# Two graph layers on one core: the softmax maxima taken over 2048 keys per head chosen on chip, and one exp over two PSUM banks

## The chip, the cores and the metric

The kernel runs on one core of a Trainium2 chip. The metric is the device time of one execution in microseconds (us). The median of three runs of the kernel before is 13,376.75 us (13,372.65 to 13,378.7). The profile shows one execution, whose span is 13,361.7 us. The engines are called PE (matrix products), DVE (vector engine), ACT (activations such as exp), POOL (GpSimd) and SP (which here only issues DMAs). PSUM, where PE writes, has eight banks of 512 float32 values on each of 128 partitions.

## The reference

Two layers run over a graph of N = 3327 nodes with 128 features. The first multiplies by the normalised adjacency matrix and its transpose and normalises. The second is attention with 128 heads of 8 dimensions, and it is nearly all of the time:

```python
q = (x @ Wq.T).reshape(d, n, h)          # d = 128 heads, n = 3327, h = 8
k = (x @ Wk.T).reshape(d, n, h)
v = (x @ Wv.T).reshape(d, n, h)
a = jnp.einsum('dnh,dmh->dnm', q, k) * scale
a = a + spatial_encoding + edge_encoding  # both are adj
a = jax.nn.softmax(a, axis=2)
out = jnp.einsum('dnm,dmh->dnh', a, v)
out = out.reshape(n, h * d)
return out @ Wo.T
```

The adjacency matrix has about five nonzero entries in a row, so it changes few scores. Its result is added to the input and normalised.

## The kernel before

**Stages.** The first layer comes first. A projection stage then makes q, k and v, 13 tiles of 256 nodes, and writes them to device memory. q and k are split into three bfloat16 parts each, stacked on 48 rows, so that one bfloat16 matmul gives the product in nearly full precision. Then comes the attention loop, and last a stage that joins results, multiplies by Wo and normalises.

**The attention loop.** Heads are taken in 32 groups of four (`g`), queries in seven blocks of 512 (`b`; the last has 255), and keys in 26 tiles of 128 (`t`). For each (g, b, t) and head a matmul (line 757) gives scores, `e_ps`, keys on partitions and queries along the bank; ACT takes exp of one bank (line 767) into `es`; and a float32 matmul (line 725) adds `es` times v into `o`. In the code the four heads are taken in two turns of the loop over `j0`; I call such a turn a half. For the last block of 255 queries, one turn takes all four heads, two to a bank.

**The maxima.** exp needs the maximum of each query's scores over all keys. A generator, `maxima()`, computes them some 76 items ahead of the exps. One item is a two-bank matmul pair (line 557), queries on partitions, and a DVE maximum over its 1024 scores (line 579). A row tile of 128 queries has 13 items for the four heads, among them two heads whose first 768 keys are stored as half sums and half differences, so that max(a, b) comes from an absolute value on ACT (line 567) and a sum on DVE (line 573). One item is taken per half. Scores use rows 0 to 49 of PE, maxima rows 64 to 111.

**From maximum to exp.** When a block's maxima are done, `lowest` (lines 516 to 528) reduces them on DVE and POOL splits the result into two bfloat16 numbers, `two`. `turn()` counts items; TURN items later `to_queries` transposes `two` on DVE (line 533), and SP stores it and loads it under the block's queries as two more rows, to be subtracted by the score matmul.

**The neighbours.** The scores above leave out adj. Beside the loop, `neighbours()` treats each node's up to 16 neighbours on POOL: 26 row tiles of nodes, each with 16 steps over keys (one indirect gather of 128 rows, line 605, and the products of lines 645 to 651), ten short steps and 16 steps over values (a gather and lines 690, 691). `by_node()` before it reorders the tables with DMAs, 256 steps. One step of the two is taken after every PACE = 4 rounds of `t`.

**Order.** Inside the loop the order of instructions on PE, ACT, DVE, POOL and SP is the order in which the code emits them (`manual_schedule`, line 702). Each engine works through its own list and stops at an instruction whose operands are not ready.

```python
            if total % PACE == 0:
                next(beside, None)
```

Of the kernel before, what the change touches and what calls it, by code (L numbers as in the profile page):

```python
# [20 lines left out]
P = 128  # L21
N = 3327
# [18 lines left out]
CW = 10  # L41
# [8 lines left out]
LEAD = 38  # L50
TURN = 8
MIXED = (0, 2)
PAIRED = 768
HALF = PAIRED // 2
SLOTS_MX = 6


def paired_from(head):

    return -head * N % (2 * D)  # L60
# [7 lines left out]
def gnn_layers(ctx: ExitStack, tc: tile.TileContext, x, adj, adjt, w_in, w_out, wq, wk, wv, wo, out):  # L68
# [10 lines left out]
    x1 = const.tile([P, NT, D], F32, name="x1")  # L79
# [10 lines left out]

    kk_d = dram.tile([2 * PARTS * H, G // 2], BF16, name="kk_d")
# [6 lines left out]
    ones_d = dram.tile([2, NP], BF16, name="ones_d")  # L98
    negmax_d = dram.tile([NG * len(BLOCKS), 2, GH * NB], BF16, name="negmax_d")
# [23 lines left out]
    with ExitStack() as c0:  # L123
# [4 lines left out]
        with ExitStack() as c1:  # L128
            first = c1.enter_context(tc.tile_pool(name="first", bufs=1))
            x0 = first.tile([P, NT, D], F32, name="x0")  # L130
            nc.sync.dma_start(x0, x.rearrange("(t p) d -> p t d", p=P))
# [107 lines left out]
            with tc.tile_pool(name="ps_mix", bufs=2, space=PSUM) as ps_mix:  # L239
# [4 lines left out]
                apply_norm(x0, stats, small, lambda t: x1[:, t, :])  # L244
                for t0 in range(0, NT, 4):
# [18 lines left out]
                most = small.tile([P, 1], F32, name="most")  # L264
                nc.vector.reduce_max(most, over, axis=AX.X)
                mark = small.tile([P, 1], F32, name="mark")
                nc.vector.tensor_scalar(mark, most, 0.0, None, op0=ALU.is_gt)
                ones = small.tile([P, 1], F32, name="ones")
                nc.vector.memset(ones, 1.0)
                marks = ps_mix.tile([1, 1], F32, name="marks", bufs=1)  # L270
                nc.tensor.matmul(marks, mark, ones, start=True, stop=True)
                nc.vector.tensor_copy(bad, marks)


# [8 lines left out]
        def load_group(g):  # L283
# [4 lines left out]
            for slot, parts in KROWS:  # L288
                src = heads[: H * parts].rearrange("r (j n) -> r j n", j=GH)
                pairs.append((k[H * slot : H * slot + H * parts, :, :N], src))  # L290
                rows = slice(64 + H * slot, 64 + H * slot + H * parts)
                for j in range(GH):
                    if j not in MIXED:
                        pairs.append((k[rows, j, :N], src[:, j]))
                        continue

                    n0 = paired_from(g * GH + j)
                    n1 = n0 + PAIRED + NB - HALF
                    at = ((g * GH + j) * N + n0) // 2
# [735 lines left out]
```

## Time and profile before

| what | value |
|---|---|
| median of three runs | 13,376.75 us |
| profiled execution, span | 13,361.7 us |
| projection stage to first maxima | 438 to 836 us |
| first maxima to last output copy | 836 to 13,121 us |
| of it the loop with exps | 924 to 13,121 us |
| last stage | 13,121 to 13,361.7 us |
| busy over the span: PE, DVE, ACT, POOL | 95%, 96%, 94%, 39% |

In a group line of the profile, "x" and a number is a count, then follow the busy time in us and the mean duration of one instruction in ns, and after the bar the idle time of the engine ahead of it and what ended it. In a timeline line the first number is the start in us and the second the length. Instructions of one engine overlap at their ends, so the step from start to start can be shorter than the length of one. A line of the table of waits has the engine, tile and line that waited, what it waited for, and the total in us, the count and the longest.

### The profile page before, as it was taken

The numbers are of one execution on the slowest core, as the hardware profiler recorded it, in microseconds if no ns is written. First come the engines' busy times: TensorE is split into PE (matmuls) and PEld (weight loads), VectorE is DVE, ScalarE is ACT, GpSimd is POOL, SyncE is SP. The second block draws the span as 40 slices with busy tenths as digits, with TensorE's granted clock in tenths as the row PEclk, the third lists the DMA queues.
The fourth block names the chain that finished last, engine by engine and source line by source line (L and its number), as shares of the span: only waits on it lengthen the run. The fifth ranks groups of instructions, "written<-read, shape, count | busy, mean of one in ns | idle before, by whom it ended". The sixth has DMA issues, their size and how long they took to land.

```text
span 13361.7 us, 325240 instructions
## 1 busy us (share of the span) xinstructions
PE 12748.4 (95%) x131844; PEld 3270.1 (24%) x131844; DVE 12885.2 (96%) x17679; ACT 12532.3 (94%) x24146; POOL 5245.4 (39%) x4554
## 2 busy tenths in 40 slices
PE   7669999999999999999999999999999999999996
PEld 3312222222222222222222222222222222222224
DVE  9779999999999999999999999999999999999996
ACT  6549999999999999999999999999999999999994
POOL 0310000004555555555555555555555555554100
PEclk8869999999999999999999999999999999999997
DMA  6753333333334443343434433434433344443203
GB/s 236 200 117 31 31 33 31 30 33 61 64 65 74 73 71 66 68 70 64 65 67 68 66 66 67 72 70 69 68 68 67 68 70 68 64 66 63 37 9 110
DMA packets 2622120, 929.24 MB, mean 70 GB/s; under 512 B 2265088, under 2 KB 2473096, under 8 KB 2613946
## 3 DMA queue, kind: packets, MB, share of 16 engines
q1 hardware_dynamic: 2488794, 398.26, 25.1%
q0 software_dynamic: 127920, 465.26, 12.7%
q10 hardware_dynamic: 3888, 44.82, 0.9%
q8 instruction: 1035, 16.96, 0.6%
q14 instruction: 483, 3.96, 0.1%
HBM read 786.21 MB, written 150.74 MB: 70 GB/s over the span
## 4 chain that ended last, share of the span: by engine, by line
PE 79%; DVE 14%; ACT 3%; DMA 2%; issue 1%; SPq 1%; POOL 0%; DVEq 0%; ACTq 0%; POOLq 0%
PE o L725 39%; PE m L557 35%; DVE mx L579 9%; PE e_ps L757 4%; ACT es L767 2%; DVE larger L573 1%; PE acc L191 1%; DMA q_d<-parts 1%; DVE top_at L201 1%; DVE top_w L200 1%; PE y L809 1%; DVE mx L571 0%; SPq L344 0%; ACT o_sb L734 0%; ACT size L567 0%
## 5 line engine op out<-in xcount | busy, mean ns | idle before, releaser
L767 ACT ACTIVATE es<-e_ps 128x512 f32<-128x512 f32 x21632 | 11447.8, 612 | 197.4 <-PE e_ps L757 126.5
L579 DVE TENSOR_REDUCE mx<-m 128x1 f32<-128x1024 f32 (+3 forms) x10816 | 10874.1, 1071 | 77.2 <-PE e_ps L757 40.2
L757 PE MATMUL e_ps<-q_st,k_st 50*128 50x512 bf16 (+1 forms) x23296 | 6661.1, 366 | 87.0 <-ACT es L767 78.8
L557 PE MATMUL m<-k_st,q_st 48*128 48x512 bf16 (+1 forms) x23296 | 6508.5, 366 | 164.1 <-DVE mx L579 84.8
L725 PE MATMUL o<-es,v 128*9 128x256 f32 (+1 forms) x83456 | 6626.7, 389 | 5.5 <-ACT o_sb L734 5.4
L557 PEld LDWEIGHTS <-q_st 48*128 48x128 bf16 x23296 | 1417.8, 94 | 5068.9 <-issue 4126.7
L725 PEld LDWEIGHTS o<-es,v 128*9 128x9 f32 x83456 | 1243.1, 88 | 4214.1 <-issue 4191.3
L526 POOL CAST two<-nm 128x16 bf16<-128x16 f32 (+1 forms) x224 | 44.1, 197 | 5621.7 <-DVE nm L520 5502.4
L757 PEld LDWEIGHTS <-k_st 50*128 50x128 bf16 (+1 forms) x23296 | 1400.2, 95 | 148.3 <-issue 112.0
L645 POOL TENSOR_TENSOR prod<-qn,near_rows 128x1024 f32<-128x1024 f32 x416 | 987.1, 2373 | 33.1 <-DMA q_st<-q_d 16.2
L573 DVE CUSTOM_DVE_ANT_0 larger<-size,m 128x384 f32<-128x384 f32 x1664 | 914.6, 550 | 66.0 <-PE e_ps L757 60.9
L567 ACT ACTIVATE size<-m 128x384 f32<-128x384 f32 x1664 | 809.6, 487 | 106.7 <-PE m L557 46.7
L691 POOL TENSOR_TENSOR acc<-acc,prod 128x1024 f32<-128x1024 f32 x390 | 887.8, 2276 | 30.6
L690 POOL TENSOR_TENSOR prod<-near_rows,s 128x1024 f32<-128x1024 f32 x390 | 772.8, 1982 | 6.8
L647 POOL TENSOR_TENSOR half<-prod 128x512 f32<-128x512 f32 x416 | 530.6, 1276 | 32.6
L571 DVE TENSOR_REDUCE mx<-m 128x1 f32<-128x128 f32 x1664 | 472.6, 284 | 27.0 <-ACT size L567 10.3
L605 POOL DMA_INDIRECT near_rows<-kn_d,near x416 | 419.0, 1007 | 112.2 <-issue 53.1
L605 POOL DMA_INDIRECT near_rows<-vn_d,near x416 | 413.4, 994 | 61.5 <-issue 16.9
L191 PE MATMUL acc<-a_t,x 128*128 128x512 f32 (+1 forms) x728 | 310.6, 583 | 63.3 <-DMA a_t<-in_adj_dram 43.3
L674 POOL TENSOR_TENSOR s<-s,gain 128x2048 f32<-128x2048 f32 x26 | 93.9, 3610 | 682.6 <-ACT s L673 682.6
L649 POOL TENSOR_TENSOR quarter<-half 128x256 f32<-128x256 f32 x416 | 254.9, 613 | 32.6
L189 ACT ACTIVATE unread<-a_t 128x3327 bf16<-128x3327 f32 x52 | 155.0, 2980 | 103.6 <-PE acc L191 38.3
(154 smaller groups left out, 3399.8 us busy)
## 6 DMA issues: line engine op xcount, KB each, us to landing
q_st<-q_d SPq DMA_DIRECT2D x2304, 32.0 KB
a_t<-in_adj_dram ACTq DMA_DIRECT2D x13, 1663.5 KB
a_t<-in_adj_dram SPq DMA_DIRECT2D x13, 1663.5 KB
a_t<-in_adjt_dram SPq DMA_DIRECT2D x13, 1663.5 KB
a_t<-in_adjt_dram ACTq DMA_DIRECT2D x13, 1663.5 KB
q_d<-parts SPq DMA_DIRECT2D x13, 1536.0 KB
k_d<-parts SPq DMA_DIRECT2D x13, 1536.0 KB
k_st<-k_d SPq DMA_DIRECT2D x32, 623.8 KB
```

Source lines behind the costliest of these rows:

```text
L557: nc.tensor.matmul(m[:, at : at + width], q[64 : 64 + KR, j, i * P : (i + 1) * P], k[64 : 64 + KR, j, c0 : c0 + width], start=True, stop=True,
L567: taken = nc.scalar.activation(sizes[-1][0], m[:, :HALF], AF.Abs)
L573: nc.vector.tensor_tensor_reduce(larger, size, m[:, :HALF], scale=1.0, scalar=LOWEST, op0=ALU.add, op1=ALU.max, accum_out=dst[0])
L579: reduced = nc.vector.tensor_reduce(dst[1] if kind == "sums" else dst[0], src, axis=AX.X, op=ALU.max)
L605: nc.gpsimd.indirect_dma_start(rows.rearrange("p d h -> p (d h)"), None, table, bass.IndirectOffsetOnAxis(ap=near[:, t, i : i + 1], axis=0))
L645: nc.gpsimd.tensor_mul(prod, qn, kg)
L647: nc.gpsimd.tensor_add(half, prod[:, :, :4], prod[:, :, 4:])
L690: nc.gpsimd.tensor_mul(prod, vg, share)
L691: nc.gpsimd.tensor_add(acc[:, :, :H], acc[:, :, :H], prod)
L725: nc.tensor.matmul(o[32 * j : 32 * j + VW, c : c + w], v4[:pt, j, t, :], e[j][:pt, c : c + w], start=t == 0, stop=t == NT - 1,)
L757: nc.tensor.matmul(bank[:pt, j, :w], k[: KR + 2, j0 + y * per + j, t * P : t * P + pt], q[: KR + 2, j0 + y * per + j, :w], start=True, sto ...
L767: nc.scalar.activation(es[:pt, :, :w], bank[:pt, :, :w], AF.Exp, scale=2.0)
```

## The change

The maxima of a head are taken over at most 2048 of its 3327 keys, those of largest norm. A squared norm per key is computed in the projection stage on POOL and stored (`size_d`). `select` halves an interval ten times on DVE, each time counting how many norms of each head lie above its middle, until at most 2048 are above; then matmuls with a triangular matrix give each chosen key its rank, and the others a place from the end, so that all 3327 keys get different places (`place_d`). `scatter` writes each head's float32 keys to their places in `kept_d` by indirect DMAs from POOL, 128 rows each, 104 to a group. The first eight heads are selected inside the projection stage, and the first group is scattered there; all 128 heads are selected at the start of the loop, one step per two halves, and the other groups are scattered beside the loop.

`parts_of_kept` loads a group's first 2048 places, splits them into bfloat16 parts on POOL, and items of kind "parts" transpose them on PE and copy them on DVE into `k_kept`. A maxima item is now one matmul for each of two heads, in rows 0 and 64, each with one bank, and two DVE maxima of 512. A row tile has eight items instead of 13; they are spread evenly over the halves. The half sums and differences are gone.

Scores of two heads also stand in rows 0 and 64, in two banks of one tile, and one exp covers both banks. The queries are loaded twice with heads placed accordingly (`q_m`, `q_e`). Score tiles go from three of one bank to two of two; maxima tiles from two of two banks to three of one. LEAD is 49 and TURN 5.

For every query `reach` times the largest left-out norm (`least`) bounds a left-out score; the last stage compares it with the maximum found (`short`) on POOL. The flag that chooses the general path is computed at the end of the last stage instead of after the first layer. x1 is stored in device memory and loaded again for the last stage.

```diff
+LEAD = 49
+TURN = 5
+KEPT = 2048
+KCUTS = KEPT // NB
+HALVINGS = 10
+SLACK = 1.001
+FIRST = 8
...
+            for y in range(2):
+                for slot, parts in KROWS:
+                    r = 64 * y + H * slot
+                    src = heads[: H * parts].rearrange("r (x y n) -> y r x n", y=2, n=N)[y]
+                    pairs.append((k[r : r + H * parts, :, :N], src))
...
+            both = [q_pool[0].tile([P, 2, NB], BF16, name=name, bufs=n) for name, n in (("q_m", 3), ("q_e", 4))]
...
+        def select(pool, bank, first_head, n, store):
+
+            sizes = pool.tile([n, NP], F32, name="sizes")
+            nc.vector.memset(sizes[:, N:], -1.0)
+            nc.sync.dma_start(sizes[:, :N], size_d[first_head * N : (first_head + n) * N].rearrange("(h n) -> h n", n=N))
+            cuts = [slice(c, c + NP // 4) for c in range(0, NP, NP // 4)]
...
+            for _ in range(HALVINGS):
+                nc.vector.tensor_scalar(middle, low, high, 0.5, op0=ALU.add, op1=ALU.mult)
+                for c, cut in enumerate(cuts):
+                    nc.vector.tensor_scalar(
+                        above, sizes[:, cut], middle, None, op0=ALU.is_gt, op1=ALU.add, accum_out=count[:, c : c + 1]
+                    )
+                    yield
...
+                turned = bank()
+                for x in range(nt):
+                    nc.tensor.matmul(turned[:, x * n : (x + 1) * n], chosen[:, x, :], ident_b[:n, :n], start=True, stop=True)
...
+        def load_choice(pool, s):
+
+            at = pool.tile([P, NT, GH], U32, name="at", bufs=2)
+            keys = pool.tile([P, GH, NT, H], F32, name="keys", bufs=2)
+            nc.sync.dma_start(at, place_d[:, s])
+            for j in range(GH):
+                head = (s * GH + j) * N
+                nc.sync.dma_start(keys[:, j], kf_d[head : head + NP, :].rearrange("(p t) h -> p t h", t=NT))
+            return at, keys
+
+        def scatter(s, at, keys):
+
+            for t in range(NT):
+                n = P if t < NT - 1 else P - 1
+                for j in range(GH):
+                    nc.gpsimd.indirect_dma_start(
+                        kept_d[s * GH + j],
+                        bass.IndirectOffsetOnAxis(ap=at[:n, t, j : j + 1], axis=0),
+                        keys[:n, j, t, :],
+                        None,
+                    )
+                    yield
...
-            def mixed_keys(s, full, sb):
...
+                            square = stage.tile([P, H, D], F32, name="square", bufs=1)
+                            nc.gpsimd.tensor_mul(square, full, full)
+                            for h in (4, 2, 1):
+                                nc.gpsimd.tensor_add(square[:, :h], square[:, :h], square[:, h : 2 * h])
+                            nc.gpsimd.dma_start(size_d[g].rearrange("(p s c) -> p s c", p=P, s=2)[:, s], square[:, 0])
...
+                if t == 0:
+                    for _ in select(chooser, lambda: ps_pr.tile([P, H * D], F32, name="pr"), 0, FIRST, store_first):
+                        pass
+                    scattered = scatter(0, *load_choice(chooser, 0))
+                elif t > 2:
+                    for _ in range(12):
+                        next(scattered, None)
...
-        ps_e = c1.enter_context(tc.tile_pool(name="ps_e", bufs=3, space=PSUM))
-        ps_m = c1.enter_context(tc.tile_pool(name="ps_m", bufs=2, space=PSUM))
+        ps_e = c1.enter_context(tc.tile_pool(name="ps_e", bufs=2, space=PSUM))
+        ps_m = c1.enter_context(tc.tile_pool(name="ps_m", bufs=3, space=PSUM))
...
+            kept = side.tile([P, GH * KEPT // P, H], F32, name="kept")
+            for j in range(GH):
+                nc.sync.dma_start(
+                    kept[:, j * KEPT // P : (j + 1) * KEPT // P, :],
+                    kept_d[s * GH + j][:KEPT, :].rearrange("(p t) h -> p t h", p=P),
+                )
...
+            nc.gpsimd.tensor_copy(parts[:, :, 0], kept)
+            nc.gpsimd.tensor_sub(left, kept, parts[:, :, 0])
+            nc.gpsimd.tensor_copy(parts[:, :, 1], left)
+            nc.gpsimd.tensor_sub(parts[:, :, 2], left, parts[:, :, 1])
+            for to, of in ((3, 0), (4, 1), (5, 0)):
+                nc.gpsimd.tensor_copy(parts[:, :, to], parts[:, :, of])
+            yield parts
...
+                                yield "maxima", g, q, mx, i, x, c
+                    late.append([1, lowest, (g, b, q_e, mx)])
+                    if b == len(BLOCKS) - 1 and g + 1 < NG:
+                        for c in range(KCUTS):
+                            for x in range(2):
+                                turn()
+                                yield "parts", g + 1, parts, x, c
...
+        def run_item(kind, g, of, *where):
+
+            banks = [ps_m.tile([P, NB], F32, name="m") for _ in range(2)]
+            kept = k_kept[g % 2]
+            if kind == "parts":
+                x, c = where
+                for y in range(2):
+                    r = slice(64 * (1 - y), 64 * (1 - y) + KR)
+                    for n in range(NB // P):
+                        at = (2 * x + y) * (KEPT // P) + c * (NB // P) + n
+                        nc.tensor.matmul(
+                            banks[y][r, n * P : (n + 1) * P],
+                            of[:, at].rearrange("p s h -> p (s h)"),
+                            ident_b,
+                            start=True,
+                            stop=True,
+                        )
...
+            mx, i, x, c = where
+            for y in range(2):
+                r = slice(64 * (1 - y), 64 * (1 - y) + KR)
+                nc.tensor.matmul(
+                    banks[y], of[r, x, i * P : (i + 1) * P], kept[r, x, c * NB : (c + 1) * NB], start=True, stop=True
+                )
...
+            for y in range(2):
+                nc.vector.tensor_reduce(mx[:, i, 2 * x + y, c : c + 1], banks[y], axis=AX.X, op=ALU.max)
...
+        def scatters():
+            loaded = load_choice(side, 1)
+            yield from scatter(1, *loaded)
+            yield "first"
+            loaded = load_choice(side, 2)
+            for s in range(2, NG):
+                now = loaded
+                for n, _ in enumerate(scatter(s, *now)):
+                    if n == GH * NT // 2 and s + 1 < NG:
+                        loaded = load_choice(side, s + 1)
+                    yield
...
+                reach = side.tile([P, HEADS], F32, name="reach")
+                prod = side.tile([P, HEADS, H], F32, name="prod", bufs=2)
+                nc.gpsimd.tensor_mul(prod, qn, qn)
...
+                nc.gpsimd.tensor_mul(acc[:, :, H + 2], reach, least)
...
+            steps = NG * NT * (2 * len(BLOCKS) - 1)
+            items = NG * (sum(-(-w // P) for _, w in BLOCKS) + 1) * 2 * KCUTS
...
+                        for x0 in range(0, 2, per):
+                            halves += 1
+                            bank = ps_e.tile([P, 2, NB], F32, name="e_ps")
+                            for x in range(per):
+                                for y in range(2):
+                                    r = slice(64 * y, 64 * y + KR + 2)
                                     nc.tensor.matmul(
-                                        bank[:pt, j, :w],
-                                        k[: KR + 2, j0 + y * per + j, t * P : t * P + pt],
-                                        q[: KR + 2, j0 + y * per + j, :w],
+                                        bank[:pt, y, x * NB // per : x * NB // per + w],
+                                        k[r, x0 + x, t * P : t * P + pt],
+                                        q[r, x0 + x, :w],
                                         start=True,
                                         stop=True,
                                     )
-                                banks.append(bank)
-                            for bank in banks:
-                                es = probs.tile([P, per, NB // per], F32, name="es")
+                            m = iter(())
+                            if taken * steps < halves * items:
+                                taken += 1
+                                m = next_item()
+                                next(m, None)
+                            es = probs.tile([P, 2, NB], F32, name="es")
+                            shape = "p y (x c) -> p y x c"
+                            if per == 1:
                                 nc.scalar.activation(es[:pt, :, :w], bank[:pt, :, :w], AF.Exp, scale=2.0)
-                                e += [es[:, j, :] for j in range(per)]
-                                next(m, None)
...
+                            if halves % 2 == 0:
+                                next(choosing, None)
+                            if halves <= GH * NT + 1 or (halves > 2 * GH * NT + 64 and put * 20 < 9 * (halves - 2 * GH * NT - 64)):
+                                put += halves > GH * NT + 1
+                                next(scattering, None)
...
+        nc.gpsimd.tensor_sub(short[:pt, t, :], n_t[:pt, :, H + 2], limit[:pt, 1])
...
+        nc.vector.tensor_scalar(mark[:, 0:1], most, worst, 0.0, op0=ALU.max, op1=ALU.is_gt)
```

## The prediction

> **What bounds the kernel now.** I read the page's first part, then the stretches, then the attention loop's own instructions, then GpSimd and its waits. Columns of the stretch row: its bounds and length in us, busy time of PE, weight loads, DVE, ACT, POOL, then PE clock, DMA share and GB/s.
>
> ```profile
> PE 12748.4 (95%) x131844; PEld 3270.1 (24%) x131844; DVE 12885.2 (96%) x17679; ACT 12532.3 (94%) x24146; POOL 5245.4 (39%) x4554
> ```
> ```profile
> 924.00:13121.00 12197.00, 12014.29 (x129887) 2895.61 (x129885) 11948.05 (x16276) 11998.22 (x23612) 5078.67 (x4379) 1.00 0.37 58
> ```
>
> The loop is 12,197 of 13,362 us, and PE, DVE and ACT are each 98% busy in it; POOL is 42% busy. So the loop has three limits close together, and each must be priced. I count in *halves*: one turn of the inner `j0` loop. There are 832 row tiles (26 per group, 32 groups) with 13 maxima items each, so 832 x 13 = 10,816 halves (the 21,632 exps are two per half); 12,197 / 10,816 = 1.128 us per half.
>
> DVE: one row tile's items start at 6003.59 and the next tile's at 6017.90, 14.31 us with DVE busy throughout; 832 x 14.31 = 11,906, plus its other work. It is the present pacemaker. PE is right behind (engine PE alone, start and length):
>
> ```profile
> 6000.29 0.39 PE L557 MATMUL m<-k_st,q_st 48*128 48x512 bf16 x1
> 6000.29 0.39 PE L757 MATMUL e_ps<-q_st,k_st 50*128 50x512 bf16 x1
> 6000.52 0.38 PE L557 MATMUL m<-k_st,q_st 48*128 48x512 bf16 x1
> 6000.52 0.38 PE L757 MATMUL e_ps<-q_st,k_st 50*128 50x512 bf16 x1
> 6000.83 0.62 PE L725 MATMUL o<-es,v 128*9 128x256 f32 x8
> 6001.38 0.39 PE L557 MATMUL m<-k_st,q_st 48*128 48x512 bf16 x1
> ```
> ```profile
> 13042.21 0.60 PE L757 MATMUL e_ps<-q_st,k_st 50*128 50x512 bf16 x2
> 13042.75 0.62 PE L725 MATMUL o<-es,v 128*9 128x256 f32 x8
> 13043.30 0.39 PE L757 MATMUL e_ps<-q_st,k_st 50*128 50x512 bf16 x1
> ```
>
> A maxima matmul on rows 64 up and a score matmul on rows 0 up start together. Steps: 0.225 to the next pair, 0.305 more to the products, 0.55 for those: 1.085 us. At the end, where no maxima are left, a half still takes 1.09: two score matmuls on the same rows run one behind the other. So what counts is *slots* of 512 columns, each holding one matmul on either set of rows.
>
> **What the change saves.** Both score matmuls of a half now share one slot (heads on rows 0 and 64), and so do the two of a maxima item. A half without an item costs 1.085 - 0.225 = 0.86, one with an item 1.085. Items fall from 13 to 8 per row tile: 6656, of which 49 run before the loop.
>
> PE: 10,816 x 0.86 = 9302; 6607 x 0.225 = 1487. Added: 248 "parts" items in the loop (eight turning matmuls each), no such row; eight weight loads at 94 ns and one more 0.085 mode gap (0.305 - 0.22) say 0.8 us, bounds 0.4 and 1.2: 198. The maxima get three one-bank buffers for two-bank items, so the second matmul of an item waits for the first reduce of the item just before: 0.225 + 0.38 (matmul) + 0.05 + 0.68 (reduce) + 0.06 = 1.39 against its turn at 1.31, 0.08 to 0.09 us. With items in 64% of halves this occurs in 0.28 of them: 10,816 x 0.28 x 0.09 = 271 (0 if the reduces are early, double if they lag). The 224 output copies and neighbour exps delaying ACT, about 100; block edges, 67. Sum 11,425, or **1.056 us per half**.
>
> ```profile
> L767 ACT ACTIVATE es<-e_ps 128x512 f32<-128x512 f32 x19200 | 10166.2, 613 | 157.7 <-PE e_ps L757 105.1 <-PE m L557 6.8 <-PE o L725 2.0
> L579 DVE TENSOR_REDUCE mx<-m 128x1 f32<-128x512 f32 x1664 | 1133.2, 681 | 15.9 <-PE e_ps L757 8.6 <-PE m L557 7.0
> L806 ACT COPY ot<-tr 128x1024 f32<-128x1024 f32 x25 | 25.0, 999 | 17.1 <-PE tr L804 17.1
> ```
>
> ACT: twelve exps fill 6010.43 to 6016.65, 0.518 each, 0.095 under their 613 ns. No exp of 1024 is in the trace; the nearest row, a two-bank copy, has 999, so 0.905 per half, 9790 us; at twice the present step, which is the most, 11,205. I take the row: hidden under PE. DVE: 13,312 reduces of 512 at 681 less the overlap, about 0.59, is 7854; 512 copies of kept keys at 0.6, 307; other 300: 8460, hidden. While the selection for all heads runs (about 40 passes of 832 columns in 192 halves, one per two halves), DVE needs 0.64 x 1.18 + 0.46 = 1.21 per half: +30.
>
> **What it puts on POOL.** GpSimd gets 31 x 104 indirect scatters in the loop, about 3224, each 128 rows. Their price is that of the gathers, also 128 rows each (first POOL view: three in a row; second: one step of the neighbour loop; third: one of its value loop).
>
> ```profile
> 3066.88 1.04 POOL L605 DMA_INDIRECT near_rows<-kn_d,near  x1 [45.06 <-PE o L725]
> 3068.22 0.97 POOL L605 DMA_INDIRECT near_rows<-kn_d,near  x1 [0.30 <-issue]
> 3069.49 0.95 POOL L605 DMA_INDIRECT near_rows<-kn_d,near  x1 [0.30 <-issue]
> ```
> ```profile
> 6000.57 1.01 POOL L605 DMA_INDIRECT near_rows<-kn_d,near  x1 [0.15 <-issue]
> ...
> 6007.14 1.01 POOL L605 DMA_INDIRECT near_rows<-kn_d,near  x1 [0.16 <-issue]
> ```
> ```profile
> 6214.78 0.98 POOL L605 DMA_INDIRECT near_rows<-vn_d,near  x1
> 6215.77 1.99 POOL L690 TENSOR_TENSOR prod<-near_rows,s 128x1024 f32<-128x1024 f32 x1
> 6217.83 2.28 POOL L691 TENSOR_TENSOR acc<-acc,prod 128x1024 f32<-128x1024 f32 x1
> 6220.26 0.99 POOL L605 DMA_INDIRECT near_rows<-vn_d,near  x1
> ```
>
> Busy 1.0 us, 1.27 to 1.34 from start to start, 1.15 to 1.20 beside other work: I take 1.2, bounds 1.0 and 1.3. Against it stands the Trainium skill, "DMA: Bandwidth & Descriptors", "Anatomy of one DMA": about 2.0 us fixed per GpSimd DMA, mostly completion. The rows show POOL going on after 1.3 at most, so I charge 1.2; what 2.0 gives is rival C.
>
> POOL's average would fit: 5079 + 3224 x 1.2 is under 11,425. But the scatters run at 9 per 20 halves, from half 272 to about 7205, and the neighbour work begins after 256 steps of four row steps, 7.43 halves each: half 1902. In these 5303 halves both are on POOL's queue, which is in written order. One neighbour row tile takes 43 steps, 320 halves. Other new POOL work is the kept keys' seven copies per group and the maxima's `two` pair, 0.036 per half, and a squared query per row tile, 5.5. In the key loop (16 steps, 119 halves) POOL needs 16 x 6.57 + 5.5 + 119 x (0.45 x 1.2 + 0.036) = 179 us where PE needs 119 x 1.056 = 126. In the value loop (119): 85 + 69 = 154 against 126. Between (82): 14 + 47 = 61, PE's 87 counts.
>
> What waits for POOL: `two` of each block is queued behind the scatters and steps; DVE's transposition of it (L533) is written TURN + 1 = 6 items later, some 9 us. Past that slack DVE stands, its reduces do not free banks, and PE, in order, stands at the next maxima matmul with scores and products behind it. Before, POOL was the one to wait there:
>
> ```profile
> POOL two L526 <- DVE nm L520: 5502.4, 212, 60.9
> ```
>
> So a row tile takes 179 + 154 + 87 - 9 (the slack, used once) = 411 us for PE's 338: 73 x 16.6 tiles = **+1204**.
>
> **The rest.** Projection stage (438 to 836, DMA share 0.91): mixed keys leave (3.9 us of DVE and two 1.04 casts on ACT, 26 times, with their POOL sums), but the first eight heads' selection stands in the queues after the first tile (some 40 passes near 0.93 and small steps, about 80 us), and squares, their store and twelve scatters make 33 us of POOL per tile for nine tiles where 30 is now spent: +80, bounds 0 and +150. First kept keys, +20. At the end x1 back, the limit on idle POOL and the last test: +10. SP: queries become 24 loads per block for 12, plus `kept`, `at` and `keys` loads and both result rows; near 48 issues at 0.5 us in a block of 53, hidden; nothing if it is not late, 5 us per block if a load waits for its scatter.
>
> Sum: 13,362 - 12,197 + 11,425 + 30 + 1204 + 110 = 13,934; the median of the runs is 15 over the span: **13,950 us**, slower by 4.3%.
>
> **Rivals.** *A, POOL never late:* the loop is PE's, 11,455: 12,745. It needs POOL's lag to be carried over a whole row tile and a scatter under 0.81 us ((204 + 5.5 + 320 x 0.036 + 144c) / 320 = 1.056). For it: a 32-byte row might be cheaper to describe than a 4 KB one; against: same count of rows. Where lag is not carried, break-even with before is c = 0.88 us: that one price decides the sign. *B, partly carried:* POOL's average of 1.23 counts, 5303 x 0.175 = 928, about 13,670; with c = 1.0, 451 and 13,200. *C, completion waits:* 2.0 per scatter gives 222 + 197 + 91 - 9 = 501 per tile, 15,440.
>
> That the last test fails and the general path runs I leave out: worked out from the reference's inputs, every query's kept maximum is at least 1.03 times its limit.
>
> **Chances.** Main case 0.57 (own range 13,550 to 14,350), A 0.18, B 0.15 with half of it on each side, C 0.05, others 0.05. Faster 0.28, within 0.2% 0.03, slower 0.69; 0.2% is about what a measurement tells from no change. The range leaves out half of A and what lies above: 12,750 to 14,400.
>
> **What would show it.** Right: scores of a half starting together; halves of 0.86 and 1.085 outside the overlap; long waits of DVE `turned` for POOL, POOL near 100% from some 3000 to 9800 us, then a faster stretch. Wrong: POOL idle before `two` throughout, scatters well under 0.88 or near 2 us, an exp above 1.05, or PE waiting often on maxima banks.

## The result and the profile after

The changed kernel takes 14,328.4 us (median of four runs, 14,319.2 to 14,334.8) against 13,374.7 for the kernel before on the same chip: ratio 1.0703, 95% interval 1.0685 to 1.0721. The forecast was 13,950, with a range of 12,750 to 14,400. The profiled execution of the kernel after spans 14,317.5 us. First its engines, busy time and share of the span, and the chain that ended last:

```profile
PE 12124.2 (85%) x124066; PEld 2962.0 (21%) x124066; DVE 9738.1 (68%) x16126; ACT 11235.4 (78%) x11615; POOL 9234.4 (64%) x8439
...
PE 48%; POOL 31%; issue 6%; DMA 3%; DVE 2%; ACT 2%; SPq 0%; POOLq 0%; ACTq 0%; DVEq 0%
```

Every engine that bounded the kernel before has less to do: DVE went from 12,885 to 9738 us, ACT from 12,532 to 11,235, PE from 12,748 to 12,124. No engine is near its span, and POOL, 64% busy over all, has 31% of the chain. An average doesn't tell where; stretches do. The columns are the bounds and length in us, then busy time and count of PE, weight loads, DVE, ACT and POOL, then the granted PE clock, the DMA share and GB/s. The first stretch lies ahead of the neighbours, the second is the stretch where the neighbours' work and the scatters share POOL.

```profile
1500.00:3000.00 1500.00, 1480.11 (x16238) 340.80 (x16236) 1160.71 (x1900) 1426.38 (x1469) 705.65 (x746) 1.00 0.42 35
3157.00:10284.00 7127.00, 5633.56 (x59422) 1259.35 (x59419) 4292.41 (x7029) 5241.43 (x5437) 5861.76 (x5297) 0.89 0.40 58
```

In the first PE is 99% busy, in the second 79%, with a granted clock of 0.89. The wide exps, one per half, count the halves: 1440 from 1500 to 3000, which is 1.042 us each; 5262 from 3157 to 10,284, 1.354 each; 2982 from 10,284 to 13,420, 1.052 each. These are the counts for ACT's exps (stretch, length, busy time and count, clock, DMA share, GB/s):

```profile
3157.00:10284.00 7127.00, 5169.42 (x5262) 0.89 0.40 58
10284.00:13420.00 3136.00, 2925.23 (x2982) 1.00 0.45 70
```

So nearly all of the loss sits in the middle stretch. POOL's busy share there looks like 82%, but the 0.3 us between two scatters isn't counted as busy. In this stretch POOL is busy for 5862 us, spends 778 between one indirect transfer and the next for "issue", and waits for other engines and for transfers for only some 330 in all. On its own timeline (start, length, then the idle time before and what ended it) there is no room; this is one step of the key loop, and further on the last scatters of a group:

```profile
5018.72 1.05 POOL L452 DMA_INDIRECT kept_d<-keys,at  x1 [0.16 <-issue]
5020.07 0.99 POOL L452 DMA_INDIRECT kept_d<-keys,at  x1 [0.30 <-issue]
5021.36 0.97 POOL L452 DMA_INDIRECT kept_d<-keys,at  x1 [0.31 <-issue]
5022.64 0.97 POOL L452 DMA_INDIRECT kept_d<-keys,at  x1 [0.30 <-issue]
5023.92 0.98 POOL L729 DMA_INDIRECT near_rows<-kn_d,near  x1 [0.30 <-issue]
5024.91 2.39 POOL L777 TENSOR_TENSOR prod<-qn,near_rows 128x1024 f32<-128x1024 f32 x1
...
5260.46 2.54 POOL L452 DMA_INDIRECT kept_d<-keys,at  x1 [0.30 <-issue]
```

A scatter takes 1.27 to 1.30 us from start to start, and the ones that move 127 rows (the last row tile of nodes, four per group of heads) take 2.53 to 2.71 and 0.3 more. Who waits for POOL is in the table of waits (total us, times, longest):

```profile
POOL two L632 <- DVE nm L626: 2058.6, 114, 65.5
ACT es L909 <- PE e_ps L894: 1555.2, 693, 47.2
DVE turned L639 <- POOL two L633: 1442.4, 85, 48.2
PE m L681 <- DVE mx L686: 1357.1, 146, 45.9
```

The first row is POOL's own wait. The other three are one wait seen three times: DVE stands at the transposition for `two`, PE at the next maxima matmul for DVE, ACT at the exp for PE. POOL's own wait for the maxima fell from 5502 us to 2059, nearly all of it outside the middle stretch. The other rows that answer to those of before, the exp, the reduce and the scatter in place of nothing (busy us and mean ns, then idle time before and what ended it):

```profile
L909 ACT ACTIVATE es<-e_ps 128x1024 f32<-128x1024 f32 (+1 forms) x9984 | 9803.4, 1024 | 1936.2 <-PE e_ps L894 1555.2
L686 DVE TENSOR_REDUCE mx<-m 128x1 f32<-128x512 f32 x13312 | 8330.2, 684 | 2526.4 <-PE m L681 2511.9
L452 POOL DMA_INDIRECT kept_d<-keys,at x3328 | 3508.4, 1054 | 1116.0 <-issue 894.4
```

And PE's instructions where POOL isn't late, to be held against the halves of the prediction:

```profile
2202.04 0.39 PE L894 MATMUL e_ps<-q_e,k_st 50*128 50x512 bf16 x2
2202.27 0.38 PE L681 MATMUL m<-k_kept,q_m 48*128 48x512 bf16 x2
2202.58 0.62 PE L858 MATMUL o<-es,v 128*9 128x256 f32 x8
2203.13 0.39 PE L894 MATMUL e_ps<-q_e,k_st 50*128 50x512 bf16 x2
2203.36 0.44 PE L681 MATMUL m<-k_kept,q_m 48*128 48x512 bf16 x2
2203.73 0.62 PE L858 MATMUL o<-es,v 128*9 128x256 f32 x8
2204.28 0.39 PE L894 MATMUL e_ps<-q_e,k_st 50*128 50x512 bf16 x2
2204.60 0.62 PE L858 MATMUL o<-es,v 128*9 128x256 f32 x8
2205.16 0.39 PE L894 MATMUL e_ps<-q_e,k_st 50*128 50x512 bf16 x2
```

Two score matmuls start together (x2), the maxima pair 0.23 later, the products 0.31 after that: 1.09 us from 2202.04 to 2203.13. The half that begins at 2204.28 has no item and takes 0.88. In the one at 2203.13 the second matmul of the item is late by 0.06, the wait for a bank.

### The profile page after: what moved, and what is told of

The parts are those of the page before. It is cut to its first block, busy times and chain, and to the rows that moved or that the text cites. A ratio compares the mean times of both kernels' runs of the same rounds, so it can differ in the third digit from the quotient of the medians.

```text
span 14317.5 us, 309098 instructions
## 1 busy us (share of the span) xinstructions
PE 12124.2 (85%) x124066; PEld 2962.0 (21%) x124066; DVE 9738.1 (68%) x16126; ACT 11235.4 (78%) x11615; POOL 9234.4 (64%) x8439
## 3 DMA queue, kind: packets, MB, share of 16 engines
q0 software_dynamic: 238080, 483.48, 14.3%
## 4 chain that ended last, share of the span: by engine, by line
PE 48%; POOL 31%; issue 6%; DMA 3%; DVE 2%; ACT 2%; SPq 0%; POOLq 0%; ACTq 0%; DVEq 0%
PE o L858 25%; PE e_ps L894 15%; POOL kept_d L452 11%; PE m L681 7%; POOL prod L777 4%; POOL acc L824 3%; POOL near_rows L729 3%; POOL prod L823 3%; DMA kept_d<-keys,at 3%; POOL half L779 2%; DVE mx L686 1%; ACT es L909 1%; POOL quarter L781 1%; POOL s L782 1%; POOL s L783 1%
## 5 line engine op out<-in xcount | busy, mean ns | idle before, releaser
L909 ACT ACTIVATE es<-e_ps 128x1024 f32<-128x1024 f32 (+1 forms) x9984 | 9803.4, 1024 | 1936.2 <-PE e_ps L894 1555.2
L686 DVE TENSOR_REDUCE mx<-m 128x1 f32<-128x512 f32 x13312 | 8330.2, 684 | 2526.4 <-PE m L681 2511.9
L858 PE MATMUL o<-es,v 128*9 128x256 f32 (+1 forms) x83456 | 6739.2, 395 | 20.2 <-issue 12.9
L894 PE MATMUL e_ps<-q_e,k_st 50*128 50x512 bf16 (+1 forms) x23296 | 4281.3, 376 | 144.7 <-ACT es L909 126.9
L452 POOL DMA_INDIRECT kept_d<-keys,at x3328 | 3508.4, 1054 | 1116.0 <-issue 894.4
L681 PE MATMUL m<-k_kept,q_m 48*128 48x512 bf16 x13312 | 2852.3, 384 | 1440.9 <-DVE mx L686 1357.1
L894 PEld LDWEIGHTS <-k_st 50*128 50x128 bf16 (+1 forms) x23296 | 1097.4, 94 | 5050.5 <-issue 5003.7
L911 ACT ACTIVATE es<-e_ps 128x1020 f32<-128x1020 f32 x832 | 819.0, 1026 | 284.6 <-PE e_ps L894 253.9
L777 POOL TENSOR_TENSOR prod<-qn,near_rows 128x1024 f32<-128x1024 f32 x416 | 986.1, 2370 | 15.9 <-DMA near_rows<-kn_d,near 7.3
L681 PEld LDWEIGHTS <-q_m 48*128 48x128 bf16 x13312 | 679.0, 97 | 73.2 <-issue 56.7
L675 DVE CAST k_kept<-m 48x512 bf16<-48x512 f32 x512 | 352.8, 689 | 120.8 <-PE m L665 108.7
```

The costliest lines, as they stand in the source:

```text
L452: nc.gpsimd.indirect_dma_start(kept_d[s * GH + j], bass.IndirectOffsetOnAxis(ap=at[:n, t, j : j + 1], axis=0), keys[:n, j, t, :], None,)
L681: nc.tensor.matmul(banks[y], of[r, x, i * P : (i + 1) * P], kept[r, x, c * NB : (c + 1) * NB], start=True, stop=True)
L686: nc.vector.tensor_reduce(mx[:, i, 2 * x + y, c : c + 1], banks[y], axis=AX.X, op=ALU.max)
L777: nc.gpsimd.tensor_mul(prod, qn, kg)
L858: nc.tensor.matmul(o[32 * j : 32 * j + VW, c : c + w], v4[:pt, j, t, :], e[j][:pt, c : c + w], start=t == 0, stop=t == NT - 1,)
L894: nc.tensor.matmul(bank[:pt, y, x * NB // per : x * NB // per + w], k[r, x0 + x, t * P : t * P + pt], q[r, x0 + x, :w], start=True, stop=True,
```

## The experiments

The theory: POOL is full where scatters and neighbours meet, and its lag, of which a fixed slack is used up once per row tile of neighbours, is handed to DVE, PE and ACT. The rivals: the time is lost to something else that the change brought (the exp over two banks, the banks of the maxima, the projection), or each scatter's completion is waited for.

### The scatters left out

```diff
             yield "first"
+            return
             loaded = load_choice(side, 2)
```

The keys of groups 2 to 31 are then never scattered; those groups read the tables of groups 0 and 1, and the flag of the last test is held at zero, so the general path doesn't run. All other work, the selection too, is as in the changed kernel.

> Leaves out the scatters of groups 2 to 31 in the loop (groups 2 to 31 take their kept keys from the tables of groups 0 and 1, and the last flag is held at zero, so maxima and output are not those of the reference); all else stays. Theory (POOL's queue is full while scatters and neighbours overlap): that stretch falls from 7127 us for 5262 halves (1.354 each) to the 1.04 to 1.05 of the stretches beside it, so the time falls by about 1610 to some 12,710 us, and the waits of DVE for POOL's two vanish (1442 us now). Rival (the wide exp, the three maxima banks or DMA traffic hold the loop back): a half stays above 1.2 us in the same stretch and the time above 13,500.

Measured: 12,750.3 us (one run) beside 13,382.5 for the kernel before. PE is 93% busy, halves take 1.05 to 1.06 us from 3000 to 12,000 us throughout, and DVE's wait for `two` is all but gone, 30 us in place of 1442:

```profile
PE 11915.1 (93%) x124066; PEld 2955.5 (23%) x124066; DVE 9730.9 (76%) x16126; ACT 11226.5 (88%) x11615; POOL 5967.1 (47%) x5319
```
```profile
DVE turned L639 <- POOL two L633: 30.3, 7, 13.1
```

So the 3120 scatters left out cost 1578 us, a mean of 0.51 each, and everything else that the change does, its projection stage included, is worth 630 us of gain. That settles sign and place, but a mean of 0.51 doesn't tell whether each scatter costs something wherever it stands or only some do.

### The same scatters at other places

All scatters stay and only their pace changes: 0.75 per half until the neighbours begin and after they end, none in the key steps, 0.65 in the short steps and 0.2 in the value steps, and more if a group would come too late for its first use.

`rate()` gives the share by the neighbours' step:

```diff
-if halves <= GH * NT + 1 or (halves > 2 * GH * NT + 64 and put * 20 < 9 * (halves - 2 * GH * NT - 64)):
+if halves <= GH * NT + 1:
+    next(scattering, None)
+elif halves > 2 * GH * NT + 64:
+    credit += rate()
+    if credit >= 1 or put * 338 < GH * NT * (halves - 154):
+        credit = max(credit - 1, 0)
+        put += 1
+        next(scattering, None)
```

> The same instructions as the changed kernel, all scatters and all neighbour steps, but the scatters are paced by what POOL does beside them: 0.75 per half before the neighbours begin, none in their key steps, 0.65 in the short steps between, 0.2 in their value steps, and more only where a group would come late. Theory (POOL's load in a stretch, not its sum, sets the time): POOL needs less than the 1.05 us of PE per half in every stretch, so the whole loop runs at 1.05 to 1.08 per half and the time is 12,750 to 13,000 us, faster than the kernel before. Rival 1 (a scatter costs the loop its time wherever it stands, by its DMA traffic or by POOL's sum): stays at 14,200 to 14,330. Rival 2 (in between, 13,300 to 13,700): lag builds up at the last block of a group, where steps come twice as often.

Measured: 12,968.1 us (12,961.3 to 12,973.6), ratio to before 0.9687 (0.9666 to 0.9707). The same instructions in another order turn a loss of 7.0% into a gain of 3.1%. The row of the wait and the same stretch as above:

```profile
DVE turned L639 <- POOL two L633: 211.5, 43, 14.6
```
```profile
3157.00:10284.00 7127.00, 6850.13 (x74460) 1571.64 (x74456) 5364.93 (x8800) 6554.02 (x6810) 5871.73 (x5238) 0.98 0.46 70
```

POOL is busy in it for 5872 us, 10 more than in the changed kernel, but 1595 of its instructions are scatters there, not 2375: 1185 instead of 704 lie between 1500 and 3157 us, and 282 come after 10,284. PE is busy for 6850 us in place of 5634. So it isn't how much POOL works that costs the time, but that it is late for `two`.

### More slack for `two`

```diff
-LEAD = 49
-TURN = 5
+LEAD = 58
+TURN = 12
```

The transposition is written seven items later (and the scatters begin 20 halves earlier).

> TURN 12 for 5 and LEAD 58 for 49: seven more items, some 11 us, between POOL's two and the transposition that waits for it; the scatters beside the loop begin 20 halves earlier, which this needs. Theory (POOL is full in the overlap): only what POOL itself still waits there can be won, 139 + 72 + 8 us of the 7127, so 14,100 to 14,300. Rival (the lag that cannot be carried is the cost, as the prediction's per-tile sum has it with 9 us of slack): 11 us more per row tile of neighbours, 16.5 tiles, about 180 us less, 14,140, and twice the slack twice the gain. Second rival (no coupling by this wait): no change, 14,328.

Measured: 14,201.9 us (14,192.0 to 14,206.2), ratio 1.0609 (1.0587 to 1.0631), some 127 us below the changed kernel; DVE's wait for `two` fell from 1442 to 1195 us. More than doubling the slack is worth 8 us for each of some 16 row tiles. That fits a slack which is used once per row tile and then gone, as in the prediction's "-9" (11 us per tile had been expected). A queue that is too full isn't cured by handing its result over later.

### 128 rows in the last scatters

```diff
-n = P if t < NT - 1 else P - 1
+n = P
```

The padding row gets a place behind the table, so the tables grow by the 2048 rows at their ends.

> The last scatter of each head moves 128 rows for 127: the padding row gets a place of its own behind the table. In the trace of the changed kernel these scatters, one in 26, take 2.55 us where the others take 0.97. Theory (the row count 127 is what makes them long, and POOL is full in the overlap): they fall to 0.97, 91 of them in the overlap, 1.58 us each, about 145 us less, 14,185. Rival 1 (long for another reason, such as being the last of a head): they stay at 2.55 and the time at 14,328. Rival 2 (shorter, but off the path): 14,328.

Measured: 14,204.7 us (14,189.2 to 14,215.9), ratio 1.0613 (1.0590 to 1.0635), 124 us less than with 127 rows. The middle stretch holds 2375 scatters in both, busy for 2347 us in place of 2495, 148 less, most of which shows in the time. The queue for software transfers moved 236,032 packets, against 238,080; 2048 over 128 scatters is 16 each, so a scatter of 127 rows takes 48 packets and one of 128 takes 32.

### Both together: a surprise

> Both edits together: scatters paced by what POOL does beside them, and 128 rows in the last scatter of a head. With the pacing alone the time was 12,968 us, DVE still waited 212 us for POOL's two, and the loop without scatters gave 12,750. Theory (POOL's queue is what is left between the two): 124 scatters of the loop are 1.58 us shorter, and part of this shows where POOL is still late, so 12,870 to 12,950. Rival (the rest is the scatters' DMA traffic or PE's own waits): 12,968 as before, within 0.2%.

Measured: 16,107.9 us, ratio 1.2024 (1.2004 to 1.2044). Two edits that gained apart lost 3100 us together. The chain of this kernel has a share that the kernels above don't have, and ACT and DVE wait for something that the profile can't name (it says "remote"):

```profile
PE 63%; another core or an unknown queue 15%; ACT 5%; POOL 4%; issue 3%; DVE 3%; DMA 1%; SPq 1%; ACTq 0%; DVEq 0%; POOLq 0%
```
```profile
ACT es L920 <- remote: 2026.5, 274, 32.7
DVE mx L688 <- remote: 1933.3, 218, 41.5
```

One such stand, by the timelines of PE, ACT and DVE:

```profile
2034.73 0.61 PE L905 MATMUL e_ps<-q_e,k_st 50*128 50x512 bf16 x2 [3.14 <-issue]
...
2041.81 0.61 PE L905 MATMUL e_ps<-q_e,k_st 50*128 50x512 bf16 x2 [5.50 <-ACT es L920]
...
2066.33 0.61 PE L905 MATMUL e_ps<-q_e,k_st 50*128 50x512 bf16 x2 [20.56 <-issue]
```
```profile
2040.73 1.02 ACT L920 ACTIVATE es<-e_ps 128x1024 f32<-128x1024 f32 x1 [6.06 <-remote]
2065.26 1.02 ACT L920 ACTIVATE es<-e_ps 128x1024 f32<-128x1024 f32 x1 [23.50 <-remote]
```
```profile
2072.99 1.29 DVE L688 TENSOR_REDUCE mx<-m 128x1 f32<-128x512 f32 x2 [28.11 <-remote]
```

Taken in order, the exp at 2065.26 reads the scores of the pair that starts at 2034.73 and ends at 2035.34 by the profile, and yet it starts 30 us later. PE's 20.56 us of "issue" are a wait for ACT: its pair at 2066.33 starts 0.05 us after that exp ends and frees the tile, as the one at 2041.81 does after the exp at 2040.73. The same holds for 235 of the 240 score pairs ahead of which PE stood for more than 2 us.

What comes late is PE's signal. ACT and DVE wait for a semaphore that only PE raises in the loop, and the trace has the times at which it rose: one is 2065.17, 0.08 us before the exp. From 1500 us on, 461 exps of this kernel start more than 3 us after their scores' end, up to 45 us, and 350 of them start within 0.1 us of such a rise (some 4% of the rises are missing from the trace). In the changed kernel, in the one with the first edit alone and in the two of the section "Pauses", no exp starts more than 2 us after its scores' end. Whether the signal is held up, or the matmuls themselves end later than the profile's modelled ends, the trace doesn't tell.

POOL meanwhile issued a scatter every 1.27 us from 2022 to 2067 without a gap. From 2041 to 2065 these were the only transfers, and took 3.0% of the DMA engines' time, so it isn't a lack of DMA bandwidth. From 1500 to 3000 us this kernel does 748 wide exps and the one with the first edit alone 1421. The edit of 128 rows alone had been harmless at 0.45 per half.

### The exp taken apart, first try

```diff
-nc.scalar.activation(es[:pt, :, :w], bank[:pt, :, :w], AF.Exp, scale=2.0)
+for y in range(2):
+    nc.scalar.activation(es[:pt, y, :w], bank[:pt, y, :w], AF.Exp, scale=2.0)
```

It stands on top of the two edits together.

> As the run with both edits, but the exp over two banks is undone: two exps of 512 into the same tile. Theory (PE's 1.05 us per half sets the time, ACT lies under it): two exps step by 0.52 each, 1.04 per half, and with output copies and the neighbours' exps ACT needs about 1.07: the loop becomes ACT's by a little, 1 to 3% slower than with the wide exp, 12,950 to 13,250. Rival (the wide exp is what the gain comes from): back to the 1.13 us per half of the kernel before, 13,700. Second rival (ACT is fully hidden either way): no difference.

Measured: 16,202.1 us, ratio 1.2096 (1.2069 to 1.2123), 0.6% above its base. With ACT standing for 2000 us for the reason above, that tells nothing of the exp. It is repeated below on a sound base.

### What one scatter costs

Every scatter is issued twice, first with 64 rows and then with all 128, to the same places with the same values.

```diff
-nc.gpsimd.indirect_dma_start(
...
-    bass.IndirectOffsetOnAxis(ap=at[:n, t, j : j + 1], axis=0),
-    keys[:n, j, t, :],
+for m in (64, n):
+    nc.gpsimd.indirect_dma_start(
...
+        bass.IndirectOffsetOnAxis(ap=at[:m, t, j : j + 1], axis=0),
+        keys[:m, j, t, :],
```

> As the run with both edits, but every scatter is issued twice, first its first 64 rows, then all 128 (the same values to the same places), to price a scatter by its rows. Theory 1 (the price is per row): the 64-row ones take about half of 0.97 us, POOL gets 3224 x 0.8 more in the loop than the 1.2 to 1.3 ms it has spare, 14,000 to 14,400 us. Theory 2 (the price is per instruction): they take 0.95 us as well, 3224 x 1.27 more, 15,500 us or more.

Measured: 20,756 us (one run). On POOL's timeline:

```profile
2000.01 0.91 POOL L455 DMA_INDIRECT kept_d<-keys,at  x1 [0.30 <-issue]
2002.28 0.97 POOL L455 DMA_INDIRECT kept_d<-keys,at  x1 [1.36 <-DMA kept_d<-keys,at]
2003.56 0.91 POOL L455 DMA_INDIRECT kept_d<-keys,at  x1 [0.30 <-issue]
```

64 rows take 0.91 us and 128 take 0.97: between these two the price is by the instruction, not by the row. The second scatter goes to the table of the one before and waits until that has landed, 2.27 us from start to start, and the next one, to another table, follows after 1.28. So the completion that rival C priced at 2.0 us exists; as a step it is 2.27. The changed kernel seldom pays it, because its scatters go round the four heads' tables: of the 2375 in its middle stretch 51 waited for an earlier one to land, 111 us in all.

### Which part of the two edits

Three runs on one chip. The first grows only the tables of the kernel with paced scatters:

```diff
-kept_d = [dram.tile([NP, H], F32, name=f"kept_d{h}") for h in range(HEADS)]
+kept_d = [dram.tile([NP + KEPT, H], F32, name=f"kept_d{h}") for h in range(HEADS)]
```

> The scatters where POOL is idle, as in the 12,968 us kernel (the last scatter of a head still moves 127 rows), and only the tables in DRAM grow by the 2048 rows that the kernel with 128 rows needed, so that the tables lie further apart. In the kernel that had both changes (16,108 us) ACT and DVE stood still for 20 to 40 us at a time. If the place of the tables causes that, this run comes to about 16,000 us. If it is the scatter of 128 rows, which leaves POOL's queue without the four scatters of 2.5 us per group, it stays at 12,940 to 13,000 us.

Measured: 12,987.2 us (one run), and no stand of ACT or DVE for "remote". So the tables' places are not the cause. The second keeps both edits and lowers the early pace:

```diff
-return 0.75
+return 0.5
```

> 128 rows in every scatter and the larger tables, scatters by phase as in the 16,108 us kernel, but 0.5 scatters per half ahead of the neighbours in place of 0.75 (0.65 between the key and value steps as there). At 0.75 POOL has 0.95 us of scatters per half of 1.04 us or less and they follow one another unbroken; at 0.5 there is 0.64 us of them and POOL has gaps. If the unbroken stream is what makes ACT and DVE stand, the stretch ahead of the neighbours is undisturbed at about 1.05 us per half and the whole comes to 12,850 to 13,000 us, unless the 0.65 per half between the steps is also too dense. If the tables or the rows are the cause whatever the pace, it stays above 14,500 us.

Measured: 13,039.2 us (13,032.4 to 13,057.6), ratio 0.9751 (0.9735 to 0.9768), and no stand either: at this pace, 128 rows do no harm. It lies a little above the range expected. It isn't the best pace, though: 788 scatters lie between 1500 and 3157 us and 1735 fell into the middle stretch, so that only 6560 halves fitted into it, against 6590 with 0.75 and 127 rows.

The third is the exp taken apart again (diff as above), now on the kernel with paced scatters and 127 rows, the only change to it.

> The 12,968 us kernel with the one exp over two banks taken apart into two exps of 512, as the kernel before has it; all else is kept. If ACT is hidden below PE either way (before: a step of 1.04 us or more for two exps of 512 each half, against PE at 1.055 with an item), the time stays within 1% of 12,968. If two exps make ACT the bound in the halves, at a step of 2 x 0.55 = 1.1 us, 10,816 halves at 1.1 plus 1060 and 250 us around them give 13,200. If ACT delays PE in turn as well, 13,500 or more.

Measured: 12,991.1 us (12,977.7 to 13,004.2), ratio 0.9711 (0.9694 to 0.9727) against 0.9687 (0.9666 to 0.9707) with one exp. The intervals overlap, and the kernel with larger tables took 12,987.2 on the same chip. ACT is busy for 11,545 us in place of 11,226, and both are under PE's 11,990:

```profile
PE 11992.5 (92%) x124066; PEld 2977.2 (23%) x124066; DVE 9731.6 (75%) x16126; ACT 11545.2 (89%) x21599; POOL 9209.6 (71%) x8439
```

The half of the change that is named in its title, one exp over two banks, is worth at most some tenths of a per cent here: ACT was not what ended last once the maxima were shorter.

### Pauses

Two runs on what the 127-row scatters had done for the kernel with 0.75. In one, POOL clears a spare buffer twice (0.8 us each) after each of a group's four last scatters, which now move 128 rows:

```diff
+if t == NT - 1 and s >= 2:
+    for _ in range(2):
+        nc.gpsimd.memset(spare, 0.0)
```

> The 16,108 us kernel (128 rows in every scatter, 0.75 per half ahead of the neighbours), and after each of the four last scatters of a group POOL clears a spare buffer twice, 2 x 0.8 us, so that POOL's queue has the same pauses of 1.6 us as with the scatters of 127 rows, at the same places, but no scatter of 127 rows. If what matters is that POOL stops issuing now and then, 12,950 to 13,050 us. If it is the scatter of 127 rows itself that clears something (it may wait until what is under way has landed, which a clear doesn't), it stays at 15,500 us or more.

In the other the early pace is 0.65, with no such pause.

> The 16,108 us kernel with 0.65 scatters per half ahead of the neighbours in place of 0.75: 0.83 us of scatters per half of 1.05. Between 0.5 (13,039 us) and 0.75 (16,108). If the stand of ACT and DVE sets in only where POOL's stream of scatters has no gap left, 12,950 to 13,050 us. If it grows with the pace (a backlog of transfers that builds up step by step), 14,000 us or more.

Measured: 12,881.6 and 12,869.2 us (one run each) beside 13,341.0 for the kernel before on this chip, ratios of 0.9656 and 0.9646. Neither shows a wait for "remote". Four pauses of 1.6 us in 104 scatters, or a pace 13% lower, remove 3200 us; a scatter of 127 rows is not needed for it. The stream's length without a gap isn't the condition by itself: the kernel with pauses issues some 35 scatters in a row between 2021 and 2066 us, and 46 at most from 1500 to 3157, against 47 in the kernel that stands, and no engine stands.

The kernel with 0.65 has the lowest ratio of all runs; it is a single run, 0.4% under the paced kernel with 127 rows, and that difference has no interval.

## Why the prediction was right, and where it was short

**The halves.** 0.86 without an item and 1.085 with one were forecast from the kernel before; 0.88 and 1.09 are in the timeline. In the stretches on both sides of the middle one the mean is 1.042 and 1.052 against 1.056. In the first 440 us, while all heads are selected, it is 1.24, where 1.21 was forecast. With the scatters left out the whole came to 12,750 us; the case in which POOL is never late had been worked out at 12,745. That the two differ by 5 us only is in part luck: the first exp came 36 us later than forecast, in that run too.

**ACT and DVE hidden.** Right: DVE is 68% and ACT 78% busy. The exp of 1024 has a mean of 1024 ns where the copy's row gave 999. The run with two exps of 512 shows the hiding: 320 us more of ACT moved the ratio by 0.0024, with intervals that overlap.

**POOL's overlap, +1204.** The mechanism was right: scatters and neighbours on one queue in written order, `two` behind them, DVE held at its transposition, slack used once per row tile. The runs with the scatters left out and at other places show it; for the slack, the run with more of it fits. Its size was the term that missed. For the 5262 halves done there the prediction has 5262 x 1.056 + 1204 = 6761 us; measured were 7127, **366 more**, which is nearly all of the 384 by which the span exceeds the sum (14,317.5 against 13,934). Two parts of the step "I take 1.2, bounds 1.0 and 1.3" make most of it. A scatter's step is 1.27 to 1.30, near the upper bound: "1.15 to 1.20 beside other work" had been read from single gathers with short instructions around them, while most scatters follow one another; 2284 x some 0.075 is about 170. And "each 128 rows" was wrong for four in 104: about 91 scatters of 127 rows in this stretch at 1.58 us more, 144; the run with 128 rows gives 124 of that back. Some 50 us are left. The prediction has nothing for waits until a scatter has landed, and they are 111 us in this stretch; that they are the 50 is not shown.

**The rest.** The first exp comes at 1061 us, 136 later than before, where +100 was forecast (80 and 20). The last stage takes 251 us against 241, the +10. Outside the middle stretch the loop was 17 us shorter than forecast.

**The rivals.** A, POOL never late, needed a scatter under 0.81 us; no run shows one below 1.26 from start to start except ahead of other work. C, 2.0 us per scatter (the Trainium skill, "DMA: Bandwidth & Descriptors", "Anatomy of one DMA"), is refuted for this kernel, whose scatters go to four tables in turn, and is what the run with doubled scatters measured, 2.27, where two in a row go to one table. B supposed that POOL's average over the stretch would count. It didn't in this order. The run with other places comes nearer to it, with 212 us of DVE's waits left, but is no test of B: it also moves scatters out of the stretch, and so lies below what B was given (13,200 to 13,670).

**What the prediction left out:** that the order is free. It took the pace of 9 in 20 as given, which was right for the time asked for, and priced no other; that the same scatters at other places would beat the kernel before was not in it.

**Still open:** why PE's signal comes up to 45 us late in the kernel with both edits. A lower pace or a few pauses of POOL remove it, while unbroken runs of scatters are as long in the kernel with pauses. What holds it up, no run shows.

## What to carry to other kernels

Before work is moved to an idle engine, look at that engine by stretches and in the order of its queue: 39% busy over the span hid a stretch where POOL was then full, and the same instructions at other places made the difference between 7.0% slower and 3.1% faster. Price a small DMA by its step from start to start in an unbroken run of them, and ask for each odd size whether it costs the same. Measure two edits together even where each gained alone; here a few pauses in POOL's scatters were then worth 3200 us.

## What the runs showed of the hardware

- An indirect scatter from GpSimd costs 1.27 us from start to start for 128 rows of 32 bytes; busy for 0.97, and 0.91 for 64 rows. One with 127 rows is busy for 2.55, and takes 48 packets in place of 32.
- In the run with doubled scatters, one to the same table as the one just before it waits until that has landed: 2.27 us from start to start.
- With 0.75 scatters of 128 rows per half, ACT and DVE stood for up to 33 and 42 us at a time, 2370 and 2230 us in all, for matmuls that had ended by the profile and whose semaphore rose late; at 0.65, or with four pauses of 1.6 us per 104 scatters, not at all.
- The exp of 1024 over two banks: 1024 ns, against 1226 for two of 512 (613 ns each in the kernel before), but there they overlap, 0.518 from start to start.
